# Front of a two-layer recurrent kernel: layernorm tiles and MLP steps issued in written order, decays one turn later, one more MLP step in each pass over the chunks' products

## The chip, the cores and the metric

The kernel runs on one core of a Trainium2 chip. Its engines are TensorE (PE in the profile, with PEld for its weight loads), VectorE (DVE), ScalarE (ACT), GpSimd (POOL) and SyncE (SP), which here only issues transfers. The metric is the time of one execution on the device in microseconds (us), taken as the median of several runs; less is better.

## The reference, cut to what matters

Two layers run on an input x of 2 x 1024 tokens with 512 features, in float32. Only the first layer is touched:

```python
xn = _layernorm(x)
# attention: 16 heads of 128, q, k, v through a causal convolution of 4 taps and silu
q, k, v = (silu(conv(xn @ W)) for W in (Wq, Wk, Wv))
alpha, beta = sigmoid(xn @ Wa + ba), sigmoid(xn @ Wb + bb)
S = alpha * S - beta * ((S k - v) k^T);  o = S q      # step by step over the tokens
s = (layernorm(o) * ln_w + ln_b) * sigmoid(xn @ Wg) @ Wo
# MLP: 512 -> 1408 -> 512
g = silu((silu(xn @ gate_w.T * gate_s) * (xn @ up_w.T * up_s)) @ down_w.T * down_s)
x = x + s * g
```

The second layer (another recurrence and a larger MLP) starts from this x.

## The kernel before, in words

The tokens are 16 tiles of 128 rows (`NTT`). The first layer has three parts, which follow each other in the code of `first_layer`.

**Layernorm (from L368).** Each tile of x is loaded by SP, `layernorm` (L74) puts statistics, mean and variance (`st`, `mv`, `ve`) on DVE, the power -1/2 (`rs`) on POOL, and the normalised tile `xn` on DVE again. `transposed` (L105) turns it on PE with the identity in `cst` and copies it by ACT into `xnT`, which holds all tokens with the features on the partitions. Between the tiles, `mlp_weights` (L351) loads the MLP's weights `gwT`, `uwT`, `dwT` from POOL's queue in four parts, kept in order there: chunk 0 ahead of the tiles, 1 and 2 after tile 3, 3 to 6 after tile 5, 7 to 10 after tile 7.

**The front (to L940).** Two things run beside each other.
- `mlp` (L399) is a generator. For each of four blocks of 512 tokens it splits `xnT` into a high and a low part (`xh` by ACT, `xl` by DVE) and then takes 11 chunks of 128 hidden features: 8 matmuls into `pg`, 8 into `pu`, `sg` (silu, ACT), `hd` (DVE), `hh` (ACT), `hl` (DVE), and 8 matmuls of the chunk before into the four banks `po`. A twelfth call of a block holds the last `po` alone; the next call starts with the block's result `g` and its store in `gd`. `some(n)` takes n calls; there are 48.
- The heads of the first three groups of two heads (`hg`) are prepared. `z` and `softplus` (L482 to L507) give the decays' logarithms, which are stored as rows in `gr` and `egr`. Then, for each `hg` and each of four windows `p` of 256 tokens of both sequences: `ahead_k` projects the keys with `wk` and convolves them (`pwk`, `ka`); `ahead_e` loads two chunks' rows of `gr` into the tile `e`, adds the mask (DVE) and takes eight exponentials (ACT), then stores `e`; `ell` calls `ahead_l` for the two chunks of the window before, four products of keys each (`pkk`), times `e` (`lt`, DVE), stored in `dl`; 14 steps of `invert` (DVE) of the group before.

**The heads' loop (from L985).** 64 units of two heads' chunks; what comes ahead of it are the loads of `wq`, `wv` and `wg` for two groups (`load_weights`, on SP), the first projections, and `within`, which loads `kb`, `ground`, `eb`, `eg`. From `order["loop"] = True` on, everything is issued in written order, with `later(n, ...)` to delay a step by n slots.

What sets the order: outside that loop, a planner in the compiler lays out each engine's queue ahead of the run. At each point of its own estimate of time it takes, of what it holds to be ready, what was written first. An engine then works its queue strictly in that order, and waits where an input is late. `keep_in_program_order` pins an instruction behind the one written before it for its engine, and the class `Ordered` does so with all calls on an engine while a condition holds. `issue_after` queues what a block writes for one engine behind a given instruction. Rooms of tiles (`tile_pool`) are used again once their last reader is done; those of the front, closed by `front.close()`, become those of the loop: `ground`, then the working tiles, then the weights.

In the code before, the order around the change is: 16 layernorm tiles; small loads; 11 MLP steps by `some(IC)`; `z` and decays; 12 turns with two MLP steps each; the rest of the MLP:

```python
        for p in range(NP):
            some(1)
            done(ahead_k(hg, p, wk["wk"], stores[hg]))
            ahead_e(hg, p, stores[hg])
            some(1)
            ell()
            for _ in zip(range(0 if hg and not p else 14), steps):
                pass
            ls.append((hg, p))
    ell()
    some(NTT * IC)
    front.close()
```

Of the kernel before, what the change touches and what calls it, by code (L numbers as in the profile page):

```python
# [22 lines left out]
P = 128  # L23
# [4 lines left out]
H = 16  # L28
# [44 lines left out]

def layernorm(nc, pool, out, in_, minus_half, eps=EPS):  # L74

    st = pool.tile([P, 6], F32, tag="ln_st", name="ln_st")
    nc.vector.bn_stats(st, in_)
    mv = pool.tile([P, 2], F32, tag="ln_mv", name="ln_mv")
    nc.vector.bn_aggr(mv, st)
    ve = pool.tile([P, 1], F32, tag="ln_ve", name="ln_ve")  # L80
    nc.vector.tensor_scalar(ve, mv[:, 1:2], eps, None, ALU.add)
    rs = pool.tile([P, 1], F32, tag="ln_rs", name="ln_rs")
    nc.gpsimd.tensor_tensor(rs, ve, minus_half[:, 0:1], ALU.pow)
    nc.vector.tensor_scalar(out, in_, mv[:, 0:1], rs, ALU.subtract, ALU.mult)

# [206 lines left out]
def first_layer(ctx, tc, a, cst, minus_half, keep, xnT, od, gd, pd, then):  # L292
# [74 lines left out]

    mlp_weights(0, 1)  # L368
    with tc.tile_pool(name="ln0", bufs=3) as lp:
        for ti in range(NTT):  # L370
            xt = lp.tile([P, D], F32, tag="xt", name=f"x_{ti}", bufs=7)
            nc.sync.dma_start(xt, a["x"][ti * P : (ti + 1) * P, :])
            xn = lp.tile([P, D], F32, tag="xn", name=f"xn_{ti}")
            layernorm(nc, lp, xn, xt, minus_half)
            b, t0 = ti // NC, (ti % NC) * P
            transposed(nc, pools["a"], ("pa", "pi")[ti % 2], xnT[:, :, b, t0 : t0 + P], xn, ident, "scalar")
            if ti in (3, 5, 7):
                mlp_weights(*{3: (1, 3), 5: (3, 7), 7: (7, IC)}[ti])

    gus = fx.tile([P, 2, IC], F32, name="gus")  # L380
    nc.sync.dma_start(gus, a["gus"])
    dsc = fx.tile([P, D], F32, name="dsc")
    nc.sync.dma_start(dsc, a["dsc0"].unsqueeze(0).to_broadcast([P, D]))
    cw = cp.tile([P, 3, H, 4], F32, name="cw")
    nc.sync.dma_start(cw, a["cw"])
    cb = cp.tile([P, 3, H], F32, name="cb")
    nc.sync.dma_start(cb, a["cb"])
    lnwb = cp.tile([P, 2], F32, name="lnwb")
    nc.sync.dma_start(lnwb, a["lnwb"])

    nc.vector.tensor_scalar(lnwb, lnwb, 0.5, None, ALU.mult)

    pl = early.enter_context(tc.tile_pool(name="at_l", bufs=1, reuse_waits="tile"))
    wab = pl.tile([P, KC, 2 * H], F32, name="wab")
    nc.sync.dma_start(wab, a["wab"].rearrange("(kc p) n -> p kc n", p=P))
    bab = pl.tile([2 * H, 1], F32, name="bab")
    nc.sync.dma_start(bab, a["bab"].unsqueeze(1))

    def mlp():  # L399

        for tt in range(NT // TB):
            b, t0 = tt // 2, (tt % 2) * TB
            xs = []
            for kc in range(KC):
                src = xnT[:, kc, b, t0 : t0 + TB]
                xh = fx.tile([P, TB], F32R, tag=f"xh{kc}", name=f"xh_{tt}_{kc}")
                nc.scalar.copy(xh, src)
                xl = fx.tile([P, TB], F32R, tag=f"xl{kc}", name=f"xl_{tt}_{kc}")
                nc.vector.tensor_tensor(xl, src, xh.bitcast(F32), ALU.subtract)
                xs.append((xh, xl))  # L410
# [4 lines left out]
            for ic in range(IC + 1):  # L415
                was = hs
                if ic < IC:
                    pgu = []
                    for n, wt in (("g", "gwT"), ("u", "uwT")):
                        pp = ps_h.tile([P, TB], F32, tag=f"p{n}", name=f"p{n}_{tt}_{ic}")  # L420
                        for kc in range(KC):
                            for i, part in enumerate(xs[kc]):
                                nc.tensor.matmul(  # L423
                                    pp,
                                    lhsT=mw[wt, ic][:, kc, :],
                                    rhs=part,
                                    start=(kc == 0 and i == 0),
                                    stop=(kc == KC - 1 and i == 1),
                                )
                        pgu.append(pp)  # L430
                    sg = ft.tile([P, TB], F32, tag="sg", name=f"sg_{tt}_{ic}")
                    nc.scalar.activation(sg, pgu[0], AF.Silu, scale=gus[:, 0, ic : ic + 1])
                    hd = ft.tile([P, TB], F32, tag="hd", name=f"hd_{tt}_{ic}")
                    nc.vector.scalar_tensor_tensor(
                        hd, in0=pgu[1], scalar=gus[:, 1, ic : ic + 1], in1=sg,
                        op0=ALU.mult, op1=ALU.mult,
                    )
                    hh = ft.tile([P, TB], F32R, tag="hh", name=f"hh_{tt}_{ic}")
                    nc.scalar.copy(hh, hd)
                    hl = ft.tile([P, TB], F32R, tag="hl", name=f"hl_{tt}_{ic}")  # L440
                    nc.vector.tensor_tensor(hl, hd, hh.bitcast(F32), ALU.subtract)
                    hs = (hh, hl)
                if was is not None:
                    for tl in range(TB // P):
                        for i, part in enumerate(was):
                            nc.tensor.matmul(  # L446
                                po[tl],
                                lhsT=part[:, tl * P : (tl + 1) * P],
                                rhs=mw["dwT", ic - 1],
                                start=(ic == 1 and i == 0),  # L450
                                stop=(ic == IC and i == 1),
                            )
                yield
            for tl in range(TB // P):
                ti = tt * (TB // P) + tl
                g = ft.tile([P, D], F32, tag="g", name=f"g_{ti}", bufs=4)
                nc.vector.tensor_tensor(g, po[tl], dsc, ALU.mult)
                last["act"] = nc.scalar.activation(g, g, AF.Silu)
                nc.scalar.dma_start(gd[ti * P : (ti + 1) * P, :], g)
# [7 lines left out]

    def load_weights(hg, names):
        w = {}
        for n in names:  # L470
            pool = pools["w"] if n != "wk" else kp if "b" in pools or not hg else fz
            w[n] = pool.tile([P, KC, 2 * P], F32, tag=n, name=f"{n}_{hg}")
            nc.sync.dma_start(
                w[n], a[n][:, hg * 256 : (hg + 1) * 256].rearrange("(kc p) n -> p kc n", p=P)
            )
        return w
# [3 lines left out]
    NCOL = NC * H * B  # L480
    some(IC)
    z = fz.tile([P, 2, NC, H, B], F32, name="z")  # L482
# [162 lines left out]
    def ahead_e(hg, p, store):  # L645
# [13 lines left out]

        def exps(i, streams):  # L660
            e, c = es[i], 2 * p + i
            col = c * H * B + hg * NS
            for s in streams:
                ACT.activation(
                    e[:, s, 1 : P + 1], e[:, s, 1 : P + 1], AF.Exp, bias=bcol[:, col + s : col + s + 1]
                )
            if s == NS - 1:
                nc.sync.dma_start(store["e"][c], e[:, :, 1 : P + 1])

        later(0, lambda: load(2 * p), lambda: load(2 * p + 1))  # L670
        later(5, lambda: masked(0), lambda: masked(1))
        later(8, *(functools.partial(exps, i, (s,)) for i in range(2) for s in range(NS)))

# [245 lines left out]
    def ell():  # L919
        if ls:  # L920
            hg, p = ls.pop(0)
            for c in (2 * p, 2 * p + 1):
                done(ahead_l(hg, c, stores[hg]))

    for hg in range(3):
        stores[hg] = new_store(hg)
        wk = load_weights(hg, ("wk",))
        steps = invert(hg - 1, stores[hg - 1]) if hg else iter(())
        for p in range(NP):
            some(1)  # L930
            done(ahead_k(hg, p, wk["wk"], stores[hg]))
            ahead_e(hg, p, stores[hg])
            some(1)
            ell()
            for _ in zip(range(0 if hg and not p else 14), steps):
                pass
            ls.append((hg, p))
    ell()
    some(NTT * IC)
    front.close()  # L940
    last_w = ctx.enter_context(ExitStack())
# [43 lines left out]
    with tc.issue_after(last["act"].ins):  # L985
        for hg in range(2):
            weights[hg] = load_weights(hg, ("wq", "wv", "wg"))
        done(made(0, 0, "q"))
# [49 lines left out]
        def joined():  # L1038
# [3 lines left out]
            later(1, *joining.rest())  # L1042

        before, joining, late, ls, steps = none, None, none, [], none
        order["loop"] = True
        for u in range(len(units) + 1):
# [40 lines left out]
            if turn4 in (0, 2) and ls:  # L1087
                hg, i_ = ls[turn4 // 2]
                later(7 if turn4 == 0 else 2, functools.partial(ahead_e, hg, i_, stores[hg]))
            if turn4 == 0:  # L1090
# [495 lines left out]
def body(ctx, tc, a, out):  # L1586
    nc = tc.nc
    keep = ctx.enter_context(tc.tile_pool(name="keep", bufs=1))
    cst = keep.tile([P, 3, P], F32, name="cst")
    nc.sync.dma_start(cst, a["consts"])  # L1590
    minus_half = keep.tile([P, NS], F32, name="minus_half")
# [94 lines left out]
```

## Time and profile before

| | |
|---|---|
| median of 3 runs | 3205.46 us (3205.04 to 3208.45) |
| the profiled execution, its own time | 3207.82 us |
| its span, first to last instruction | 3206.0 us |
| PE busy | 3154.4 us (98%) |
| DVE, ACT, POOL busy | 2145.9, 1249.3, 829.2 us |
| first transpose on PE | 12.73 us |
| first matmul of the MLP | 17.79 us |
| first matmul of `z` (in the chain) | 88.72 us |
| first projection of the loop (`pwq`) | 412.04 us |
| x loads, median from issue to landing | 5.8 us |
| `e<-gr`, median from issue to landing, whole run | 4.1 us |
| mean granted PE clock | 0.995 |

The profile is one execution; its instructions carry the line of the kernel or of a helper (L131 is the call inside `Ordered`, so there the names of tiles tell more than the line). An entry reads: start, duration, engine, line, operation, out<-in, shape, and in brackets how long the engine stood idle ahead of it and who released it. PEclk is the clock that PE was granted, as a share of full speed. The times of matmuls overlap, since they are pipelined and their ends are modelled; what counts is the distance from one group to the next.

### The profile page before, as it was taken

To read this page: it belongs to the slowest core of one execution; us is meant where nothing else is said; L and a number is where in the kernel's file an instruction comes from. 1 tells how busy PE (TensorE), PEld (TensorE's weight loads), DVE (VectorE), ACT (ScalarE), POOL (GpSimd) and SP (SyncE) were. 2 spreads that over 40 slices of the span, in tenths; PEclk is the share of its full clock that TensorE was granted. 3 is DMA by queue.
4 is the path that set the end of the run, shared out by engine and by line. 5 is a ranking of instruction groups with operands and counts; after the bars stand their busy time and mean duration, and the time that the engine had idled before them with its cause. 6 is when DMAs were issued, how large, how long until landed. Compare 5 with 4: busy or idle time off the path is not lost.

```text
span 3206.0 us, 38256 instructions
## 1 busy us (share of the span) xinstructions
PE 3154.4 (98%) x12454; PEld 1953.3 (61%) x12454; DVE 2145.9 (67%) x4294; ACT 1249.3 (39%) x2267; POOL 829.2 (26%) x1204
## 2 busy tenths in 40 slices
PE   7999999999999999999999999999999999999998
PEld 6566756666666666666666644555555555555554
DVE  4566568787777868675554454676777666776677
ACT  3475445555555555434333300322222222322223
POOL 2000022222222222222222210333233333333222
PEclk9999999999999999999999999999999999999999
DMA  6244333444444543444334365110001100110014
GB/s 182 63 138 113 98 103 96 117 133 127 124 113 121 147 120 98 117 126 104 96 90 135 108 191 163 35 38 27 27 27 33 33 27 27 33 33 27 27 36 131
DMA packets 501798, 287.40 MB, mean 90 GB/s; under 512 B 207328, under 2 KB 443616, under 8 KB 501600
## 3 DMA queue, kind: packets, MB, share of 16 engines
q1 hardware_dynamic: 493600, 272.12, 30.2%
q0 software_dynamic: 5696, 8.65, 0.9%
q10 hardware_dynamic: 2304, 4.20, 0.4%
q8 instruction: 99, 1.62, 0.2%
q14 instruction: 99, 0.81, 0.1%
HBM read 183.90 MB, written 88.34 MB: 85 GB/s over the span
## 4 chain that ended last, share of the span: by engine, by line
PE 87%; DVE 5%; DMA 3%; ACT 2%; issue 2%; SPq 1%; POOL 0%; DVEq 0%; ACTq 0%; POOLq 0%
PE po L131 15%; PE pua L131 7%; PE pga L131 7%; PE pgate L131 6%; PE pwk L131 6%; PE pwq L131 5%; PE pwv L131 5%; PE zw L131 4%; PE pgc L131 3%; PE puc L131 3%; PE jpo L210 3%; PE pg L423 2%; PE pu L423 2%; PE po L446 2%; PE pub L131 2%
## 5 line engine op out<-in xcount | busy, mean ns | idle before, releaser
L131 DVE TENSOR_TENSOR acc<-acc,po 128x512 f32<-128x512 f32 x408 | 278.3, 682 | 208.3 <-PE po L131 207.6
L131 PEld LDWEIGHTS po<-w_d,i 128*128 128x128 f32 x1024 | 194.5, 190 | 142.6 <-issue 111.2
L131 PE MATMUL po<-w_d,i 128*128 128x256 f32 (+1 forms) x1024 | 275.3, 392 | 0.0
L131 PE MATMUL pgate<-xnT,wg 128*128 128x512 f32 x512 | 245.7, 593 | 0.0
L131 PE MATMUL pwq<-xnT,wq 128*128 128x512 f32 x512 | 245.1, 593 | 0.0
L131 PE MATMUL pwv<-xnT,wv 128*128 128x512 f32 x512 | 243.0, 593 | 1.8 <-ACT gate L131 1.8
L131 PE MATMUL pua<-xq,w_u 128*128 128x512 f32 x512 | 240.6, 592 | 0.0
L131 PE MATMUL pga<-xq,w_g 128*128 128x512 f32 x512 | 240.6, 592 | 0.0
L131 PE MATMUL pwk<-xnT,wk 128*128 128x512 f32 x512 | 238.0, 595 | 1.7 <-ACT ka L131 1.7
L131 ACT COPY g<-pga 128x512 f32<-128x512 f32 x96 | 56.2, 585 | 447.3 <-PE pga L131 447.3
L131 DVE SCALAR_TENSOR_TENSOR v<-prewv,cw,v 128x512 f32<-128x512 f32 x192 | 169.0, 881 | 63.2 <-ACT v L131 53.8
L131 PEld LDWEIGHTS po<-w_d,s 128*128 128x128 f32 x720 | 136.8, 190 | 95.4 <-issue 77.2
L131 ACT COPY w<-zw 128x128 f32<-128x128 f32 x192 | 50.6, 264 | 359.5 <-PE zw L131 359.5
L131 DVE TENSOR_TENSOR rr<-rr,zw 128x128 f32<-128x128 f32 x192 | 54.8, 285 | 198.1 <-PE zw L131 196.6
L131 PE MATMUL po<-w_d,s 128*128 128x256 f32 x720 | 184.8, 379 | 0.0
L131 POOL TENSOR_TENSOR ot<-ot,gate 128x512 f32<-128x512 f32 x64 | 86.6, 1354 | 344.3 <-ACT ot L131 314.9
L131 POOL TENSOR_TENSOR rs<-rs,minus_half 128x4 f32<-128x4 f32 x64 | 64.4, 1007 | 428.9 <-DVE rs L131 389.9
L131 DVE SCALAR_TENSOR_TENSOR ka<-prewk,cw,ka 128x512 f32<-128x512 f32 x192 | 147.9, 772 | 36.7 <-ACT ka L131 25.7
L131 PEld LDWEIGHTS zw<-rr,ground 128*128 128x128 f32 x512 | 96.8, 191 | 123.8 <-issue 101.6
L131 DVE SCALAR_TENSOR_TENSOR q<-prewq,cw,q 128x512 f32<-128x512 f32 x192 | 159.1, 829 | 13.8 <-ACT q L131 7.3
L131 ACT ACT_TABLE_LOAD x115 | 147.5, 1283 | 14.5 <-PE pr L131 11.3
L131 PEld LDWEIGHTS zw<-w,ground 128*128 128x128 f32 x768 | 111.3, 192 | 65.7 <-issue 54.4
(249 smaller groups left out, 6686.3 us busy)
## 6 DMA issues: line engine op xcount, KB each, us to landing
e<-gr SPq DMA_DIRECT2D x64, 256.0 KB, 4.1
de<-e SPq DMA_DIRECT2D x64, 256.0 KB, 2.7
dk<-ka SPq DMA_DIRECT2D x32, 512.0 KB, 2.8
kb<-dk SPq DMA_DIRECT2D x64, 256.0 KB, 3.4
eb<-de SPq DMA_DIRECT2D x64, 256.0 KB, 3.0
eg<-egr SPq DMA_DIRECT2D x64, 256.0 KB, 3.8
od<-ot SPq DMA_DIRECT2D x64, 256.0 KB, 2.1
wt<-w SPq DMA_DIRECT2D x768, 16.0 KB, 1.9
```

The costliest lines, as they stand in the source:

```text
L131: i = getattr(self.engine, name)(*args, **kw)
L210: matmul(po, lhsT=ot[:, h, :], rhs=self.wo[h], start=(h == h0), stop=(h == H - 1))
L423: nc.tensor.matmul(pp, lhsT=mw[wt, ic][:, kc, :], rhs=part, start=(kc == 0 and i == 0), stop=(kc == KC - 1 and i == 1),)
L446: nc.tensor.matmul(po[tl], lhsT=part[:, tl * P : (tl + 1) * P], rhs=mw["dwT", ic - 1], start=(ic == 1 and i == 0), stop=(ic == IC and i == 1),
```

## The change

Five things are done in `first_layer`; `body` only gives up its load of `cst`.

1. The layernorm's tiles and the first 11 MLP steps go through `Ordered`, so on PE, DVE, ACT and POOL they are issued as written. `layernorm` now returns its last operation (`xn`) for the caller to place: for tiles 0 to 3 it comes after the statistics of the next tile, for the others at once. From tile 4 on, each tile but the last is followed by one MLP step (`some(1)`) and then by its transposes. x is loaded two tiles ahead in the text; `cst` comes after the first two tiles, `gus` and `dsc` after the fourth; the other small loads stay behind the tiles.
2. `ahead_e` returns its loads, masks and exponentials as lists. In the front the loads are done in their turn, the masks and exponentials at the start of the next turn. In the loop `decays` places them as before.
3. `ell` takes one MLP step between the two halves, and one more comes after the last turn.
4. The first six weight loads of the loop (`wq`, `wv`, `wg` of two groups) are issued from POOL instead of SP.
5. The halving of `lnwb` is pinned behind the front on DVE.

```diff
-def layernorm(nc, pool, out, in_, minus_half, eps=EPS):
+def layernorm(vector, gpsimd, pool, out, in_, minus_half, eps=EPS):
...
-    nc.vector.tensor_scalar(out, in_, mv[:, 0:1], rs, ALU.subtract, ALU.mult)
+    return lambda: vector.tensor_scalar(out, in_, mv[:, 0:1], rs, ALU.subtract, ALU.mult)
...
+    first = {"on": True}
+    ordered = {
+        n: Ordered(tc, getattr(nc, n), lambda: first["on"])
+        for n in ("tensor", "vector", "scalar", "gpsimd")
+    }
...
-                nc.scalar.copy(xh, src)
+                ordered["scalar"].copy(xh, src)
...
+        xts = [load_x(ti) for ti in range(2)]
+        nc.sync.dma_start(cst, a["consts"])
+        mlp_weights(0, 1)
+
+        late = None
+        for ti in range(NTT):
+            if ti + 2 < NTT:
+                xts.append(load_x(ti + 2))
+            xn, end = normed(ti, xts[ti])
+            if ti < 4:
+                if late:
+                    turned(*late)
+                late = ti, xn, end
+                if ti == 3:
+                    turned(*late)
+                    gus = fx.tile([P, 2, IC], F32, name="gus")
+                    nc.sync.dma_start(gus, a["gus"])
+                    dsc = fx.tile([P, D], F32, name="dsc")
+                    nc.sync.dma_start(dsc, a["dsc0"].unsqueeze(0).to_broadcast([P, D]))
+            else:
+                end()
+                if ti < NTT - 1:
+                    some(1)
+                turned(ti, xn, lambda: None)
+            if ti in (3, 5, 7):
+                mlp_weights(*{3: (1, 3), 5: (3, 7), 7: (7, IC)}[ti])
...
-    some(IC)
+    first["on"] = False
...
-        later(0, lambda: load(2 * p), lambda: load(2 * p + 1))
-        later(5, lambda: masked(0), lambda: masked(1))
-        later(8, *(functools.partial(exps, i, (s,)) for i in range(2) for s in range(NS)))
+        return (
+            [lambda: load(2 * p), lambda: load(2 * p + 1)],
+            [lambda: masked(0), lambda: masked(1)],
+            [functools.partial(exps, i, s) for i in range(2) for s in range(NS)],
+        )
...
                 done(ahead_l(hg, c, stores[hg]))
-
+                if c == 2 * p:
+                    some(1)
+
+    of_e = ()
...
         for p in range(NP):
+            for step in of_e:
+                step()
             some(1)
             done(ahead_k(hg, p, wk["wk"], stores[hg]))
-            ahead_e(hg, p, stores[hg])
+            loads, *of_e = ahead_e(hg, p, stores[hg])
+            of_e = itertools.chain(*of_e)
+            for step in loads:
+                step()
             some(1)
             ell()
...
+    for step in of_e:
+        step()
+    some(1)
     ell()
     some(NTT * IC)
+
+    tc.keep_in_program_order(nc.vector.tensor_scalar(lnwb, lnwb, 0.5, None, ALU.mult))
     front.close()
...
-            weights[hg] = load_weights(hg, ("wq", "wv", "wg"))
+            weights[hg] = load_weights(hg, ("wq", "wv", "wg"), nc.gpsimd)
...
+        def decays(hg, p):
+            for n, some_steps in zip((0, 5, 8), ahead_e(hg, p, stores[hg])):
+                later(n, *some_steps)
```

More of the change, by code (lines that the diff above doesn't have):

```diff
@@ L71, in rep @@
     return ap.unsqueeze(1).to_broadcast([ap.shape[0], n, ap.shape[1]])
-def layernorm(nc, pool, out, in_, minus_half, eps=EPS):
+def layernorm(vector, gpsimd, pool, out, in_, minus_half, eps=EPS):
     st = pool.tile([P, 6], F32, tag="ln_st", name="ln_st")
-    nc.vector.bn_stats(st, in_)
+    vector.bn_stats(st, in_)
     mv = pool.tile([P, 2], F32, tag="ln_mv", name="ln_mv")
-    nc.vector.bn_aggr(mv, st)
+    vector.bn_aggr(mv, st)
     ve = pool.tile([P, 1], F32, tag="ln_ve", name="ln_ve")
-    nc.vector.tensor_scalar(ve, mv[:, 1:2], eps, None, ALU.add)
+    vector.tensor_scalar(ve, mv[:, 1:2], eps, None, ALU.add)
     rs = pool.tile([P, 1], F32, tag="ln_rs", name="ln_rs")
-    nc.gpsimd.tensor_tensor(rs, ve, minus_half[:, 0:1], ALU.pow)
-    nc.vector.tensor_scalar(out, in_, mv[:, 0:1], rs, ALU.subtract, ALU.mult)
+    gpsimd.tensor_tensor(rs, ve, minus_half[:, 0:1], ALU.pow)
+    return lambda: vector.tensor_scalar(out, in_, mv[:, 0:1], rs, ALU.subtract, ALU.mult)
 def softplus(nc, pool, out, x, sign, tags):
@@ L366, in mlp_weights @@
             mw["dwT", ic] = w[:, ic - c0, :]
[L368 to L397, printed above, removed]
+    first = {"on": True}
[3 more added lines that the diff above has]
+    }
     def mlp():
@@ L406, in mlp @@
                 xh = fx.tile([P, TB], F32R, tag=f"xh{kc}", name=f"xh_{tt}_{kc}")
-                nc.scalar.copy(xh, src)
+                ordered["scalar"].copy(xh, src)
                 xl = fx.tile([P, TB], F32R, tag=f"xl{kc}", name=f"xl_{tt}_{kc}")
-                nc.vector.tensor_tensor(xl, src, xh.bitcast(F32), ALU.subtract)
+                ordered["vector"].tensor_tensor(xl, src, xh.bitcast(F32), ALU.subtract)
                 xs.append((xh, xl))
@@ L422, in mlp @@
                             for i, part in enumerate(xs[kc]):
-                                nc.tensor.matmul(
+                                ordered["tensor"].matmul(
                                     pp,
@@ L431, in mlp @@
                     sg = ft.tile([P, TB], F32, tag="sg", name=f"sg_{tt}_{ic}")
-                    nc.scalar.activation(sg, pgu[0], AF.Silu, scale=gus[:, 0, ic : ic + 1])
+                    ordered["scalar"].activation(sg, pgu[0], AF.Silu, scale=gus[:, 0, ic : ic + 1])
                     hd = ft.tile([P, TB], F32, tag="hd", name=f"hd_{tt}_{ic}")
-                    nc.vector.scalar_tensor_tensor(
+                    ordered["vector"].scalar_tensor_tensor(
                         hd, in0=pgu[1], scalar=gus[:, 1, ic : ic + 1], in1=sg,
@@ L438, in mlp @@
                     hh = ft.tile([P, TB], F32R, tag="hh", name=f"hh_{tt}_{ic}")
-                    nc.scalar.copy(hh, hd)
+                    ordered["scalar"].copy(hh, hd)
                     hl = ft.tile([P, TB], F32R, tag="hl", name=f"hl_{tt}_{ic}")
-                    nc.vector.tensor_tensor(hl, hd, hh.bitcast(F32), ALU.subtract)
+                    ordered["vector"].tensor_tensor(hl, hd, hh.bitcast(F32), ALU.subtract)
                     hs = (hh, hl)
@@ L445, in mlp @@
                         for i, part in enumerate(was):
-                            nc.tensor.matmul(
+                            ordered["tensor"].matmul(
                                 po[tl],
@@ L456, in mlp @@
                 g = ft.tile([P, D], F32, tag="g", name=f"g_{ti}", bufs=4)
-                nc.vector.tensor_tensor(g, po[tl], dsc, ALU.mult)
-                last["act"] = nc.scalar.activation(g, g, AF.Silu)
+                ordered["vector"].tensor_tensor(g, po[tl], dsc, ALU.mult)
+                last["act"] = ordered["scalar"].activation(g, g, AF.Silu)
                 nc.scalar.dma_start(gd[ti * P : (ti + 1) * P, :], g)
@@ L466, in some, with load_x, normed, turned @@
             pass
-    def load_weights(hg, names):
+    with tc.tile_pool(name="ln0", bufs=3) as lp:
+        def load_x(ti):
+            xt = lp.tile([P, D], F32, tag="xt", name=f"x_{ti}", bufs=7)
+            nc.sync.dma_start(xt, a["x"][ti * P : (ti + 1) * P, :])
+            return xt
+        def normed(ti, xt):
+            xn = lp.tile([P, D], F32, tag="xn", name=f"xn_{ti}")
+            return xn, layernorm(ordered["vector"], ordered["gpsimd"], lp, xn, xt, minus_half)
+        def turned(ti, xn, last):
+            last()
+            b, t0 = ti // NC, (ti % NC) * P
+            transposed(types.SimpleNamespace(**ordered), pools["a"], ("pa", "pi")[ti % 2], xnT[:, :, b, t0 : t0 + P], xn, ident, "scalar")
+        xts = [load_x(ti) for ti in range(2)]
[23 more added lines that the diff above has]
+                mlp_weights(*{3: (1, 3), 5: (3, 7), 7: (7, IC)}[ti])
+    cw = cp.tile([P, 3, H, 4], F32, name="cw")
+    nc.sync.dma_start(cw, a["cw"])
+    cb = cp.tile([P, 3, H], F32, name="cb")
+    nc.sync.dma_start(cb, a["cb"])
+    lnwb = cp.tile([P, 2], F32, name="lnwb")
+    nc.sync.dma_start(lnwb, a["lnwb"])
+    pl = early.enter_context(tc.tile_pool(name="at_l", bufs=1, reuse_waits="tile"))
+    wab = pl.tile([P, KC, 2 * H], F32, name="wab")
+    nc.sync.dma_start(wab, a["wab"].rearrange("(kc p) n -> p kc n", p=P))
+    bab = pl.tile([2 * H, 1], F32, name="bab")
+    nc.sync.dma_start(bab, a["bab"].unsqueeze(1))
+    def load_weights(hg, names, queue=nc.sync):
         w = {}
@@ L472, in load_weights @@
             w[n] = pool.tile([P, KC, 2 * P], F32, tag=n, name=f"{n}_{hg}")
-            nc.sync.dma_start(
+            queue.dma_start(
                 w[n], a[n][:, hg * 256 : (hg + 1) * 256].rearrange("(kc p) n -> p kc n", p=P)
@@ L658, in masked, with exps @@
             DVE.tensor_tensor(e[:, :, 1 : P + 1], e[:, :, 1 : P + 1], rep(mask, NS), ALU.add)
-        def exps(i, streams):
+        def exps(i, s):
             e, c = es[i], 2 * p + i
             col = c * H * B + hg * NS
[L663 to L666, printed above, removed]
+            ACT.activation(
+                e[:, s, 1 : P + 1], e[:, s, 1 : P + 1], AF.Exp, bias=bcol[:, col + s : col + s + 1]
+            )
             if s == NS - 1:
                 nc.sync.dma_start(store["e"][c], e[:, :, 1 : P + 1])
-        later(0, lambda: load(2 * p), lambda: load(2 * p + 1))
-        later(5, lambda: masked(0), lambda: masked(1))
-        later(8, *(functools.partial(exps, i, (s,)) for i in range(2) for s in range(NS)))
+        return (
+            [lambda: load(2 * p), lambda: load(2 * p + 1)],
+            [lambda: masked(0), lambda: masked(1)],
+            [functools.partial(exps, i, s) for i in range(2) for s in range(NS)],
+        )
     def ahead_l(hg, c, store):
@@ L1088, in first_layer @@
                 hg, i_ = ls[turn4 // 2]
-                later(7 if turn4 == 0 else 2, functools.partial(ahead_e, hg, i_, stores[hg]))
+                later(7 if turn4 == 0 else 2, functools.partial(decays, hg, i_))
             if turn4 == 0:
@@ L1589, in body @@
     cst = keep.tile([P, 3, P], F32, name="cst")
-    nc.sync.dma_start(cst, a["consts"])
     minus_half = keep.tile([P, NS], F32, name="minus_half")
```

## Prediction, made before the change was run

> **What bounds the kernel now.** The page has TensorE (PE) busy for 98% of the span, so a gain can come only from stretches in which PE stands still or runs slow. All of the change lies ahead of the heads' loop, and that begins at 412.04 us, with the first projection by `wq`. So I asked first for the busy time of the engines in the stretches up to 412, cut where the chain shows a new kind of work:
>
> ```profile
> core 0: us, PE busy (x) PEld busy (x) DVE busy (x) ACT busy (x) POOL busy (x), PEclk, DMA share, GB/s
> 0.00:88.70 88.70, 71.82 (x321) 56.92 (x322) 40.89 (x93) 29.89 (x48) 20.28 (x41) 0.98 0.56 165
> 88.70:320.00 231.30, 229.56 (x894) 149.94 (x894) 141.60 (x243) 142.63 (x234) 13.11 (x62) 1.00 0.40 109
> 320.00:356.00 36.00, 29.46 (x107) 20.74 (x106) 29.44 (x68) 21.77 (x40) 0.00 (x0) 0.81 0.36 108
> 356.00:412.00 56.00, 56.00 (x241) 44.87 (x240) 21.62 (x45) 14.61 (x23) 3.45 (x5) 1.00 0.29 71
> ```
>
> The first and the third stretch have idle PE, and the third has a granted clock of 0.81. The ends of matmuls are modelled, so I count work instead of trusting busy time. The chain of work gives the pace of each kind where nothing waits (start, us, what):
>
> ```profile
> 55.18 1.86 PE pg L423 x8
> 57.04 1.87 PE pu L423 x8
> 58.91 1.85 PE po L446 x8
> ...
> 93.76 3.55 PE pz L488 x8
> ...
> 166.60 6.87 PE pwk L131 x16
> ...
> 219.01 0.89 PE pkk L131 x8
> ```
>
> So an MLP step is 1.86 + 1.87 + 1.85 = 5.58, one `ahead_k` 6.87, one `pkk` tile 0.89, all `pz` 4 x 3.55 = 14.2; the timeline has the transposes of two tiles in 1.03, so 0.52 a tile. Work by stretch, from the matmuls that each holds (tile queries for pg, pu, po, pwk, pkk, 8 or 16 to a group as in the chain):
> - to 88.7: 11 pg/pu pairs (41.0), 10 po (18.5), 16 tiles (8.2) = 67.7. Lost: 21.0, of which 12.7 ahead of the first transpose.
> - to 320: 21 steps (117.2), pz and what hangs on it (17), 11 `ahead_k` (75.6), 20 pkk (18) = 228. Lost: 3.5.
> - to 356: 24 + 17 + 18 matmuls of the MLP (13.7), 1 `ahead_k` (6.9), 4 pkk (3.6) = 24.2. Lost: 11.8.
> - to 412: ten steps of pure MLP, 56.0. Lost: nothing.
>
> Together 36 us. The waits of the first 130 us, then of 130 to 412 (total, times, longest), say on whom:
>
> ```profile
> DVE ln_st L77 <- DMA x<-in_x: 16.5, 8, 4.4
> PE ptr L114 <- DVE xn L84: 13.6, 2, 12.7
> ```
> ```profile
> PE po L446 <- DVE hl L441: 2.8, 1, 2.8
> ```
>
> VectorE's (DVE's) own timeline shows why the first transpose is at 12.7:
>
> ```profile
> 5.09 0.18 DVE L79 BATCH_NORM_AGGREGATE ln_mv<-ln_st 128x2 f32<-128x6 f32 x1
> 7.30 0.69 DVE L77 BATCH_NORM_STATS2 ln_st<-x 128x6 f32<-128x512 f32 x1 [2.03 <-DMA x<-in_x]
> 7.92 0.14 DVE L81 TENSOR_SCALAR ln_ve<-ln_mv 128x1 f32<-128x1 f32 x1
> ...
> 12.14 1.44 DVE L84 TENSOR_SCALAR xn<-x,ln_mv,ln_rs 128x512 f32<-128x512 f32 x3
> ```
>
> Tile 0 has its mean and variance at 5.3, but the planner put the next tiles' statistics ahead of its `ve` and `xn`: the queue stands behind transfers that landed later than planned.
>
> **Part 1, layernorm and the first 11 steps in written order.** Queue of DVE, with the durations above (stats 0.69, aggregate 0.18, `ve` 0.14, `xn` 0.54, POOL's power 0.55): stats 0 at 4.3, `ve` 0 by 5.4, stats 1 at 6.9 (x_1 is now issued ahead of `cst`; it landed at 7.3), `xn` 0 done by 8.5, then 1.56 a tile: `xn` 3 done at 12.3. POOL then issues three weight loads (2.4 us in this trace, at 14.50 to 16.88) ahead of the power of tile 4, so `xn` 4 ends at 15.4; it stands ahead of `xl` on DVE. `xl` 0 ends at 16.1 and the MLP starts there, against 17.79 now. Its first pg and pu are 3.7 us of work. Here a rule matters. The clock: rows of this trace grant 0.50 at 20 to 22 us and 0.72 at 22 to 24, though PE had worked since 12.7. The Trainium skill, "TensorE: Matmul & The Clock Gate", Part 1, says that the array starts at half rate and is freed after about 3.4 us of sustained work. By the rule, PE is freed before 20 and pg/pu end at 22.4; by the row (five slow microseconds after the MLP starts) they end nearer 23.5. I take 22.4, and 23.5 for the range. From there ten turns of 5.58 + 0.52, and two more tiles: 84.5. A turn's other engines fit: DVE 0.75 + 0.69 + 1.55 = 3.0 us of 6.1; ScalarE (ACT) 0.69 + 0.62 + 0.58 = 1.9. `xn` of the next tile is ready 4.6 us after pu, its transposes come 8.5 after. The weights for steps 3 to 6 are issued after the power of tile 5, at about 24, and needed at 33 (gate) and 35 (up): at 390 GB/s (the rate at 26 to 42 us now) 1 MB takes 2.7 us, so they land at about 29.5 and 32; the 13.8 and 16.4 us to landing of now are with both big sets and x under way at once. **Gain: 88.7 - 84.5 = 4.2**, between 1 and 7.
>
> **Part 2, MLP steps spread, and decays a turn later.** Before, 11 steps, then two in each of 12 turns, then the other 13 calls (the generator has 48, four of them only a po) in one block. After, `ell` takes one between its two halves, and nothing is left for the block. No work is added. What moves: the 11.8 us of 320 to 356, where the last `ahead_k`, the second inversion, the last masks and exponentials and the block change of the MLP (new `xh`, `xl`, four `g`) fell together with DVE 82% busy and PE out of order only by plan. After, the last block change comes in the first turn of the third group of heads, which has no inversion steps; and behind the last `ahead_k` stand three steps, 16.8 us, where the chain from it to `pkk` is 5 us (0.6 + 0.8 copies, 3 x 0.75 taps, 1.06 silu). A turn is 6.87 + 3 x 5.58 + 1.78 = 25.4 us of PE, against about 21 of DVE. The masks (24 x 0.69), exponentials (96 x 0.39) and table loads (1.28) are the same in number; their place a turn later keeps DVE from standing behind `e<-gr` (6.6 us of waits in 130 to 412), but the 3.5 us lost from 88.7 to 320 bound what that brings, and I count nothing. The last turn's masks now come after the loop, and the end has only one step and a po as cover, so I leave 4 us lost there (1 to 12). **Gain: 11.8 - 4 = 8.** With it goes the clock: 0.50 was granted from 338 to 350 after PE waited.
>
> **Part 3, the six weight loads of the loop go from SP's queue to POOL's.** SP now:
>
> ```profile
> 375.63 0.76 SPq L473 DMA_DIRECT2D wq<-in_wq  x1
> ...
> 414.79 0.37 SPq L473 DMA_DIRECT2D wg<-in_wg  x1
> ```
>
> Five of six are issued by 381, 31 us ahead of use, so their room is free long before the last step; the sixth waits 33.6 us for the last stores of `g` and holds up SP, with `kb` and `ground` behind it. On POOL it holds up the memsets of `pre` and `eg` and the halo copies, which the loop's first taps need 5 us later than PE's first 6.87 us: covered. The Trainium skill, "DMA: Bandwidth & Descriptors", section "SWDGE vs HWDGE vs iDMA", speaks against it: plain copies belong on SP or ACT, whose setup is faster. The rows agree on the sign (512 KB: 5.5 us to landing from SP, 7.1 and more from POOL; issue 0.37 and 0.86). With cover the rule costs nothing; without, 2 us. SP freed early brings at most the 1.3 us that PE idles from 430 to 500. **Together: 0.5 lost** (-1 to +3). The moved `lnwb` (0.36 us of DVE), `cst`, `gus`, `dsc` and small loads lie under the same cover: 0.
>
> **Sum.** 4.2 + 8 - 0.5 = 11.7. The profiled execution took 3207.8 (span 3206.0); 3207.8 - 11.7 = 3196.1, and the median of the runs is 2.4 lower: **3193.8**. From 412 on the order is the same and only shifts. About 0.2% (6.4 us) can be told from no change, so "same" is 3199 to 3212.
>
> **Rivals.**
> - *The first stage gains nothing* (12%): x arrivals rule it, for which the 16.5 us of waits speak; against it, most fall after 25 us, when the planner had run ahead of the transfers. 3193.8 + 4.2 = 3198.
> - *The end keeps its stall* (16%): the planner still lays out masks and `pkk` by its own landing times; it pulls MLP steps forward while the decays are not ready, and the end is bare. For it: DVE waits on `e<-gr` in every turn now. 3193.8 + 8 = 3202, no change.
> - *Slower* (12%): at the switch to the loop, the weight loads stand on POOL behind `ground`'s memset (3.31 us, released at 408.31 by the last pu) and behind the last stores of `g`, which the sixth load waited for (414.79). Then `wq` lands at 414.8 + 1.0 + 7 to 9.6 = 423 to 425: 11 to 13 us of idle PE and, by the 12 us at 0.50 above, 6 more. 3193.8 + 19 = 3213. It breaks even at 11.7, and is slower beyond 18. Against it: five loads didn't wait so.
> - *Likeliest* (60%): 3187 to 3199.
>
> Range 3185 (startup 7, end 1, loop's start 1.3) to 3207 (over the stall's case, part of the loads'). Faster 0.72, same 0.16, slower 0.12.
>
> **What would show it.** First transpose near 9 and `pz` from 82 to 87; no stretch of over 3 us with PE idle between there and the end of the front; last po near 400; `wq` landed before that. Wrong if PE waits for gwT or uwT in turns 2 to 4, if DVE's `e` masks stand between hd and hl while PE waits, or if the first pwq comes later than 2 us after the last MLP matmul.

## The result, and the profile after

The changed kernel takes 3190.24 us (median of 6 runs, 3187.01 to 3192.71), the kernel before 3206.86 us in the same comparison (6 runs, 3205.04 to 3210.47): a ratio of 0.9949, with a 95% interval of 0.9939 to 0.9959. That is 16.6 us faster, where the forecast was 11.7. The profiled execution took 3191.48 us, with a span of 3188.9. The loop starts at 392.9 us instead of 412.0, so 19.1 us had been won there; 17.1 are left in the span. The first 120 us of the loop hold about as much idle PE as before (2.1 us against 2.0), and the last 2 us are no more than two profiles of one kernel differ by (3188.9 and 3186.3 for the changed kernel).

The same view as before, busy time in stretches, cut at the first `pz` (88.4) and at the first `pwq` (392.9):

```profile
core 0: us, PE busy (x) PEld busy (x) DVE busy (x) ACT busy (x) POOL busy (x), PEclk, DMA share, GB/s
0.00:88.40 88.40, 77.56 (x344) 61.42 (x344) 47.02 (x98) 32.72 (x53) 20.66 (x41) 1.00 0.58 172
88.40:320.00 231.60, 230.10 (x896) 153.18 (x896) 140.20 (x238) 140.62 (x235) 11.51 (x52) 1.00 0.36 99
320.00:356.00 36.00, 36.00 (x156) 27.00 (x155) 29.86 (x68) 19.30 (x32) 1.74 (x9) 1.00 0.28 87
356.00:392.90 36.90, 36.90 (x167) 28.13 (x166) 21.70 (x43) 18.70 (x30) 6.88 (x7) 1.00 0.43 110
```

The third stretch had 29.46 us of busy PE at a clock of 0.81; it now has 36.00 at 1.00, and nothing is left idle from there to the loop. Counted as work with the durations of the forecast: up to `pz` there are 12 pg/pu pairs (44.8), 11 po (20.4) and 16 tiles (8.2), so 15.1 us are lost of 88.4 (before 21.0). `pz` itself starts no earlier than before, because one more pair and po stand ahead of it. From `pz` to the loop there are 32 pairs (119.4), 33 po (61.1), `pz` and what hangs on it (17), 12 `ahead_k` (82.4) and 24 `pkk` (21.4), 301.3 together, so 3.2 us are lost of 304.5 (before 3.5 + 11.8). The two parts have won 5.9 and 12.1; the 1.1 us to 19.1 are within the rounding of these durations.

The start on DVE and PE (timelines of each):

```profile
3.40 0.69 DVE L132 BATCH_NORM_STATS2 ln_st<-x 128x6 f32<-128x512 f32 x1 [3.40 <-DMA x<-in_x]
...
4.42 0.68 DVE L132 BATCH_NORM_STATS2 ln_st<-x 128x6 f32<-128x512 f32 x1
...
5.42 0.54 DVE L132 TENSOR_SCALAR xn<-x,ln_mv,ln_rs 128x512 f32<-128x512 f32 x1
7.89 0.69 DVE L132 BATCH_NORM_STATS2 ln_st<-x 128x6 f32<-128x512 f32 x1 [1.93 <-DMA x<-in_x]
```
```profile
6.56 1.09 PE L132 MATMUL ptr<-cst,xn 128*128 128x128 f32 x4 [6.56 <-DMA cst<-in_consts]
...
14.45 0.80 PE L132 MATMUL pg<-xh,gwT 128*128 128x512 f32 x1 [1.32 <-ACT xh L132]
15.46 0.79 PE L132 MATMUL pg<-xl,gwT 128*128 128x512 f32 x1 [0.22 <-DVE xl L132]
...
19.04 0.58 PE L132 MATMUL pu<-xl,uwT 128*128 128x512 f32 x1
19.46 0.40 PE L132 MATMUL pu<-xh,uwT 128*128 128x512 f32 x1
...
20.87 0.60 PE L132 MATMUL ptr<-cst,xn 128*128 128x128 f32 x4
```

The first transpose now waits for the identity, not for statistics; it comes at 6.56 instead of 12.73, the MLP at 14.45 instead of 17.79, and the first step ends at 20.87. From there a turn takes 6.0 us, up to the last at 81.10. Of the 15.1 us still lost, 12.4 lie ahead of the MLP's first matmul (14.45 less four tiles of 0.52) and 2.7 in the first step (6.42 against 3.73 of work).

The switch to the loop, on POOL and on SP:

```profile
375.34 0.80 POOL L505 DMA_DIRECT2D wq<-in_wq  x1 [15.97 <-ACT sg L132]
376.13 0.77 POOL L505 DMA_DIRECT2D wv<-in_wv  x1
387.69 3.30 POOL L995 MEMSET ground<- 128x3840 f32 x1 [10.79 <-PE pu L132]
390.94 0.75 POOL L505 DMA_DIRECT2D wg<-in_wg  x1
```
```profile
384.63 14.13 SPq L720 DMA_DIRECT2D dl<-lt  x12
402.21 0.59 SPq L732 DMA_DIRECT2D ll<-dl  x1
```

`wq` and `wv` are out 17 us ahead of use. The other four loads do stand behind the memset of `ground`, as the slower rival had it, but the loop needs them last. SP meanwhile issues stores of `lt` from 384.6 to 398.8. This line turned out to be the one that matters.

### The profile page after: what moved, and what is told of

The parts are those of the page before. It is cut to its first block, busy times and chain, and to the rows that moved or that the text cites. A ratio compares the mean times of both kernels' runs of the same rounds, so it can differ in the third digit from the quotient of the medians.

```text
span 3188.9 us, 38235 instructions
## 1 busy us (share of the span) xinstructions
PE 3148.8 (99%) x12454; PEld 1950.8 (61%) x12454; DVE 2147.2 (67%) x4294; ACT 1251.4 (39%) x2269; POOL 832.4 (26%) x1210
## 4 chain that ended last, share of the span: by engine, by line
PE 76%; DVE 5%; issue 2%; ACT 1%; DMA 1%; SPq 1%; POOL 0%; DVEq 0%; ACTq 0%; POOLq 0%
PE po L132 15%; PE pua L132 7%; PE pga L132 7%; PE pgate L132 6%; PE pwq L132 5%; PE pwv L132 5%; PE pwk L132 4%; PE zw L132 4%; PE pgc L132 3%; PE puc L132 3%; PE jpo L211 3%; PE pub L132 2%; PE pgb L132 2%; PE pr L132 2%; PE pks L132 1%
```

## The experiments

The theory (A): the start and the stall are separate gains that add; the decays' place and the queue of the six loads are worth about nothing. Rivals: the stall is an accident of the plan, which any change ahead of it dissolves (C), or the decays' later place, not the spread steps, takes the stall away (B). Each run is set beside runs of the kernel before that were taken with it.

### The start alone

Before, with `layernorm`, x loads, transposes and 11 steps as in item 1 of the change (and item 5), nothing else:

```diff
+    first = {"on": True}
+    ordered = {n: Ordered(tc, getattr(nc, n), lambda: first["on"]) ...}
...
-    some(IC)
+    first["on"] = False
```

> The kernel before with the layernorm and the first 11 MLP steps in written order, nothing else of the change but the place of the lnwb halving. Theory A (two separate gains: the start of PE, and the MLP steps spread so that no stretch is left without cover): only the start is gained. Time lost by PE up to the first pz falls from 21.0 to about 15 us, the stall between 320 and 356 stays: 6 us faster than before, 3201. Rival C (the stall of 320 to 356 was an accident of the plan, which any change ahead of it dissolves): 18 us faster, 3189.

Measured: 3199.69 us against 3206.34, 0.9977 (0.9968 to 0.9987): 6.6 us faster. The stall stays, in the stretches of 20 us:

```profile
320.00:340.00 20.00, 14.34 (x62) 10.66 (x60) 15.75 (x35) 16.88 (x33) 0.00 (x0) 0.91 0.52 129
340.00:360.00 20.00, 18.20 (x69) 14.66 (x70) 16.31 (x40) 5.89 (x10) 0.00 (x0) 0.83 0.29 78
```

C falls: the start is a gain of its own, of the size that the trace of the whole change shows (5.9).

### The MLP steps spread, alone

The kernel before with item 3 of the change only (`spread_only`):

```diff
                 done(ahead_l(hg, c, stores[hg]))
+                if c == 2 * p:
+                    some(1)
...
+    some(1)
     ell()
```

> The kernel before with one MLP step more in each ell and one behind the last turn, nothing else. Theory A: the start stays (first transpose at 12.7, 21 us lost to the first pz), the front's stall goes: 12 us faster than before, 3195. Rival B (the gain of the second half comes from the masks and exponentials a turn later, which keep DVE from standing behind their loads): no change, 3207. Rival C gives 12 here too.

Measured: 3203.38 us, 0.9991 (0.9984 to 0.9997): 3.0 us, a quarter of what was expected. Yet the stall is gone: PE is busy for 20.00 us in both stretches from 320 to 360. The time is lost again at the loop's start, on PE and on SP:

```profile
397.14 1.05 PE L131 MATMUL pkk<-ka 128*128 128x128 f32 x8
406.15 9.15 PE L131 MATMUL pwq<-xnT,wq 128*128 128x512 f32 x16 [7.96 <-DMA wq<-in_wq]
```
```profile
396.26 6.27 SPq L687 DMA_DIRECT2D dl<-lt  x8
402.64 0.39 SPq L473 DMA_DIRECT2D wq<-in_wq  x1
```

PE's last work of the front begins at 397.1, and `wq`, issued by SP only after the stores of `lt`, lands at 406.2. The projection then takes 9.15 us instead of 7.03 (its time in the changed kernel), at a granted clock of 0.50:

```profile
404.00:408.00 4.00, 1.85 (x2) 0.84 (x3) 0.00 (x0) 0.00 (x0) 0.00 (x0) 0.50 1.02 330
```

7.96 + 2.1 = 10.1 us go there. A's last clause falls. In its place (A2): the spread steps and POOL's queue belong together.

### POOL's queue alone, and both together

```diff
-            weights[hg] = load_weights(hg, ("wq", "wv", "wg"))
+            weights[hg] = load_weights(hg, ("wq", "wv", "wg"), nc.gpsimd)
```

> The kernel before with only the six weight loads moved to POOL. By theory A2 the queue matters only where the MLP steps are spread, since in the kernel before five of six were issued 31 us ahead of use: no change, 3206 to 3208, the stall of 320 to 356 in place. The prediction's sum gave 0.5 us more. If POOL's queue is worth something by itself (SP no longer held 33.6 us by the sixth load): up to 1.3 us less.

> The kernel before with one MLP step more in each ell and one behind the last turn, and the six weight loads on POOL; layernorm and decays as before. Theory A2: the stall of the front is gone and wq is there in time: 3206.3 - 12 = 3194. Rival (the decays a turn later are needed too): wq in time but a stall of 5 us or more in the last turns: 3199 or more. If only the queue was wrong in spread_only, PE's wait of 8.0 us for wq must be gone.

POOL alone: 3209.7 us, 1.0009 (1.0001 to 1.0017), 3.3 us slower; its first `pwq` is at 411.9, as before, so nothing is late there. Its profile has the span of the kernel before, 3206.0; where the 3 us go stays open. Both: 3192.97 us against 3207.59, 0.9958 (0.9946 to 0.9971), 14.6 faster. `pwq` starts at 398.75 and PE's only wait from 130 to 420 is 1.4 us for `ka`. So the two changes gain -3.3 and +3.0 us alone and +14.6 together: A2 holds.

### The whole change with the loads back on SP

```diff
-            weights[hg] = load_weights(hg, ("wq", "wv", "wg"), nc.gpsimd)
+            weights[hg] = load_weights(hg, ("wq", "wv", "wg"))
```

> The changed kernel with the six weight loads of the loop back on SP's queue. Theory A2 (formed after spread_only: the MLP steps and the POOL queue belong together, since with the steps spread the stores of lt fill SP's queue to the end of the front and wq is issued behind them): wq lands some 8 us after the last matmul of the front, PE waits and comes back at half clock: 3190 + 11 = 3201. Theory of the prediction (the queue is worth 0.5 us either way, its room being free early): 3190.

Measured: 3193.96 us, 0.996 (0.9946 to 0.9974), 3.7 and 5.9 us above the changed kernel's two medians (3190.24, 3188.09), and 7.4 above `warm` (3186.58, below), which was measured together with it and has the loads on POOL; not 11. PE waits 4.24 us for `wq`, which SP gets to issue between two groups of stores:

```profile
384.86 8.30 SPq L720 DMA_DIRECT2D dl<-lt  x8
393.26 0.39 SPq L505 DMA_DIRECT2D wq<-in_wq  x1
394.40 3.16 SPq L720 DMA_DIRECT2D dl<-lt  x4
```
```profile
397.58 8.83 PE L132 MATMUL pwq<-xnT,wq 128*128 128x512 f32 x16 [4.24 <-DMA wq<-in_wq]
```

The mechanism is the one of A2, with a smaller price: `wq` was issued one group of stores earlier, so the wait is about half as long. The clock fell here too, only for less time: 0.50 is granted from 399 to 401, and the projection takes 8.83 us instead of 7.03. 4.24 + 1.8 = 6.0 us go there.

### The whole change without the spread steps

```diff
-                if c == 2 * p:
-                    some(1)
...
-    some(1)
```

> The changed kernel without the MLP step in ell and without the one behind the last turn; the start in written order, the decays a turn later and the weight loads on POOL stay. Theory A: a stall comes back in the front's last turns, and a block of pure MLP follows it: 10 to 12 us slower than the changed kernel, 3201. Rival B: no change against the changed kernel, 3190. Rival C: no change either.

Measured: 3205.18 us, 0.9993 (0.9984 to 1.0001), 15 to 17 us above the changed kernel. The stall is back (14.84 and 18.28 us busy from 320 to 360, clock 0.89 and 0.77), and now it is `lt` that PE waits for:

```profile
PE pkk L132 <- DVE lt L132: 6.0, 3, 3.5
```

This kernel is also 5.5 us slower than the start alone, though it only adds the decays' later place and POOL's queue. Alone these cost 2.3 and 3.3. Over all runs the stall follows the spread steps: the eight profiles with them have PE busy for all 40 us from 320 to 360, the five without them for 32 to 33.5.

### The decays a turn later, alone, and back in their turn

Before with item 2 of the change only (`decays_only`):

> The kernel before with only the masks and exponentials a turn later. Theory A: nothing gained, since the stall stays where the MLP steps give no cover, 3205 to 3209. Rival B: the stall goes, 12 us faster, 3195, with the waits of DVE on e<-gr (8 us in the front) near zero. Rival C: the plan changes here too, so about 12 faster.

Measured: 3208.61 us, 1.0005 (0.9997 to 1.0014). The stall is only moved, from a wait for `hl` to one for `lt`, which reads exponentials that now come later (waits of 130 to 420, then the stretches):

```profile
PE pkk L131 <- DVE lt L131: 6.3, 3, 3.6
```
```profile
320.00:340.00 20.00, 17.60 (x71) 11.79 (x70) 19.36 (x44) 15.01 (x25) 0.00 (x0) 1.00 0.32 89
340.00:360.00 20.00, 14.51 (x57) 10.78 (x56) 14.90 (x38) 10.86 (x21) 0.00 (x0) 0.83 0.53 140
```

B falls. The other way round, the whole change with masks and exponentials in their own turn:

```diff
-            loads, *of_e = ahead_e(hg, p, stores[hg])
-            of_e = itertools.chain(*of_e)
-            for step in loads:
+            for step in itertools.chain(*ahead_e(hg, p, stores[hg])):
                 step()
```

> The changed kernel with each turn's masks and exponentials in its own turn. Theory A2: their place is worth nothing or costs, as decays_only said (3208.6 against 3206.3): 3188 to 3191, PE losing at most 4 us between the first pz and the first pwq. Rival B: 5 us or more of PE waits come back in the front, 3195 or more.

Measured: 3187.04 us, 0.9938 (0.9925 to 0.995). That is no slower than the changed kernel (0.9949 and, run again, 0.9939); PE is busy throughout from 320 to the loop, and DVE only 9.79 us of the 20 from 320 on. The later place brings nothing. Against the changed kernel's medians it seems to cost 1 to 3 us; against `warm` (below), measured together with this run and with the later place, it costs nothing (3186.58). These runs can't tell.

### A warm PE at the start

The changed kernel with a few matmuls of ones (dummies), which nobody reads, in PE's gaps of the first 13 us (`warm`). The expectation's "page" is the one on the clock that the prediction cites.

```diff
+        wz = ft.tile([P, TB], F32, tag="sg", name="wz")
+        ordered["vector"].memset(wz, 1.0)
+        wp = ps_h.tile([P, TB], F32, tag="pg", name="wp")
...
+                ordered["tensor"].matmul(wp, lhsT=wz[:, :P], rhs=wz, start=True, stop=True)
```

> The changed kernel with six matmuls of ones more on PE, three ahead of the first transpose, two behind the second tile's and one behind the fourth's, whose result nobody reads. The first MLP step took 6.4 us (14.45 to 20.87) in the changed kernel, ten of its matmuls at 0.43 us. By the page's rule of a clock freed after some 3.4 us of sustained work, they run at 0.23 us now and the step ends by 19.7: 1.2 us less in the profile, too little for the medians (3189 to 3190). By the rival (the clock is not what holds the step, its inputs xh and xl are): it ends at 20.9 as before.

Measured: 3186.58 us, 0.9939 (0.9927 to 0.9951). The first step ended at 20.09, 0.8 earlier than in the changed kernel and 0.4 later than expected, and by the interval no gain is shown. The matmuls of the MLP start at full pace, 0.26 to 0.34 us apart, and fall to 0.43 at 15.87; the stretches show the clock:

```profile
12.00:14.00 2.00, 1.23 (x3) 0.19 (x1) 0.64 (x3) 1.97 (x4) 1.43 (x3) 1.00 1.07 340
14.00:16.00 2.00, 1.33 (x5) 0.73 (x6) 2.00 (x5) 1.98 (x3) 0.00 (x0) 0.99 1.18 323
16.00:18.00 2.00, 2.00 (x5) 1.58 (x6) 0.42 (x1) 0.52 (x2) 0.00 (x0) 0.50 1.24 345
```

From 12.7 to 14.7, between its last dummy and the first `xl`, PE did a single matmul (0.49 us); the clock was lowered about a microsecond after that gap, when PE had full work again. The last kernel puts dummies into that gap too, and has the decays in their turn:

> The changed kernel with each turn's masks and exponentials in its own turn and with eight matmuls of ones between the first transposes (three ahead of them, two after the first tile's, one after the second's, two after the fourth's). In warm the clock fell back to 0.50 at 16 us, after PE had idled at 12.7 to 14.7; with the denser row it should stay at 1.00 and the first MLP step end near 18.8 (20.9 in the changed kernel, 20.1 in warm). Sum: decays in turn 3 us, clock 2 us: 5 us under the changed kernel, 3185. If the masks' place was noise: 3188.

> The changed kernel once more, on the same chip as the next two, as their measure: 3190, as before (3187 to 3193).

Measured together: 3186.33 us, 0.9933 (0.9921 to 0.9946), and the changed kernel 3188.09 us, 0.9939 (0.9925 to 0.9952). Here the pace stays full (timeline of PE):

```profile
14.57 0.47 PE L132 MATMUL pg<-xh,gwT 128*128 128x512 f32 x1
15.55 0.50 PE L132 MATMUL pg<-xl,gwT 128*128 128x512 f32 x1 [0.51 <-DVE xl L132]
...
19.33 0.40 PE L132 MATMUL pu<-xl,uwT 128*128 128x512 f32 x1
19.56 0.60 PE L132 MATMUL ptr<-cst,xn 128*128 128x128 f32 x4
20.70 0.47 PE L132 MATMUL pg<-xh,gwT 128*128 128x512 f32 x1 [0.54 <-DMA gwT<-in_gwT]
```

The step ends at 19.56, 1.3 us earlier, not at 18.8 as expected, because `xl` comes as late as before. So the cold clock costs 1.3 us of the first step, but this kernel doesn't keep them. The second step waits for its weights, 0.54 us for `gwT` and 1.26 for `uwT`, and ends at 27.87, where the changed kernel's ends at 26.88; `pz` starts at 89.4 instead of 88.4. From the second step on, the transfers hold the start back in this profile, not the clock. 1.8 us less than the changed kernel is the lowest median of the study, but the intervals overlap, and the first steps don't explain it.

## Why the prediction held, and where it failed

**Part 1 (4.2 expected; 5.9 by the trace, 6.6 alone).** The mechanism was right: DVE's queue no longer stands behind late statistics. Three terms were mis-sized.

- The arrival of x. x_1 was counted to land at 6.9; issued ahead of `cst` it landed with x_0 (statistics at 3.40 and 4.42). But x_2 came only at 7.89, so `xn` 4 keeps 0.6 us of that lead (14.81, counted 15.4). The MLP starts at 14.45, not 16.1, mostly because its first matmul needs `xh` alone; the first with `xl` is at 15.46.
- The clock. The forecast read five slow microseconds after the MLP's start out of the rows of before. That was a misreading: there the MLP's first matmuls go at full pace (0.23 to 0.34 us apart from 18.71 to 19.78, granted 1.00 up to 19), and the slow stretch comes later, from 19.7 to 23.1, after PE had stood still from 16.5 to 17.8. In the changed kernel the matmuls do run at half pace from the first one on, for 5.0 us, 4.0 of them after the last gap (15.46 to 19.46), against the 3.4 that the Trainium skill, "TensorE: Matmul & The Clock Gate", Part 1, gives for sustained work. The step took 6.4 us, counted 6.3 by the rule and 7.4 by the row; its end at 20.87 instead of 22.4 is owed to the earlier start.
- The weights for steps 3 to 6. Counted to land at 29.5 and 32, they landed at 31.7 (`gwT`) and 34.7 (`uwT`). That was no wait, but only by half a microsecond: `uwT` is first used at 35.22.

The turns of 6.1 held (6.0). `pz` was expected from 82 to 87 and came at 88.4, since the forecast left out the pair and the `po` that now stand ahead of it (3.73 + 1.85); that moves work and loses none.

**Part 2 (8 expected; 12.1 by the trace).** The 11.8 us of the stall went, and of the 4 us left for a bare end nothing came; the other 3.5 became 3.2. Taking the stall for a matter of cover (too few MLP steps beside the chain through DVE) fits the runs: the whole change without the spread steps brings it back, the spread alone removes it. The decays, "I count nothing", brought nothing; alone they made `pkk` wait for `lt`, so that the place needs the spread steps as cover.

**Part 3 (0.5 lost expected; by the traces it is worth 6 in the whole change and 10 beside the spread alone).** This is the step that failed: "Five of six are issued by 381, 31 us ahead of use, so their room is free long before the last step." This is true of the order before only. There a block of pure MLP, 56 us with few stores, ended the front, and SP reached the loads early. With the steps spread, `ell` works up to the end, SP issues stores of `lt` until PE has done its last step, and a load written behind them comes 8 us (spread alone) or 4 us (whole change) too late; the lower clock after the wait costs 2 us more. The second part created the need for the third, and by costing them one by one on the queue of before I missed it. That the sum still came out is luck: the change contains both, so the missing term never showed. The rule that the prediction set against the move (plain copies belong on SP or ACT) speaks of setup; POOL alone, 3.3 us slower, agrees with it in sign, though where these 3 us go is open. In the whole change it pointed the wrong way: the place in the queue, 4 to 8 us of PE's wait, weighed more than the 0.4 us of issue and the few us of landing.

**The sum.** The start alone 6.6, spread with POOL 14.6, decays -2.3 (not clear of noise): 18.9 if they add; measured 16.6 and, the second time, 18.3. It fits within the few us by which these medians vary.

**The rivals.** The start that gains nothing and the end that keeps its stall didn't come. The slower one had the place right (four loads behind `ground`'s memset) and the consequence wrong: `wq` and `wv` were taken early, and the last four are needed only behind 7 us each of projections.

## What to carry to other kernels

Before a move of work is costed, lay out anew each queue that the moved steps write to: a load that was early behind a quiet stretch is late when the stretch fills with stores, and the engine with the slower issue but an empty queue can then be the better one. Here a stall of the critical engine beside a long chain on another was cured by spreading independent work over the turns, not by a later place for part of the chain. Test such parts alone and in pairs: -3.3 and +3.0 alone were +14.6 together.

## What was not expected of the hardware

The granted clock in the profile seems to miss the cold start. In the changed kernel its stretches from 14 to 20 us say 1.00 while the MLP's matmuls start 0.43 us apart; after 19.46 the same matmuls are 0.23 apart. In the run with dummies the same pace of 0.43 stands beside a granted 0.50. In the kernel before, 16 transposes at 12.73 take 3.73 us under a granted 1.00, as slow as eight at 20.21 under 0.50 (1.91 us). At the start of a kernel the distance between matmuls is the surer reading.

A gap also takes the clock away late: in the run with dummies, after some 2 us of mostly idle PE (12.7 to 14.7), the pace halved at about 15.9, in the middle of dense work, and was full again at about 19.4. The same lag stands in the kernel before (gap from 16.5 to 17.8, low from 19.7) and with the loads back on SP (gap from 393.3 to 397.6, low from 398.3). Worked out from rows of one microsecond (with the loads back on SP 0.65, 0.50, 0.50 and 0.64 from 398 to 402, so low from 398.3 to 401.7), the low stretch lasts 3.4 us in each of these three, 6.8 after the wait for `wq` with the spread alone (403.4 to 410.2), and 13.6 in the stall of before (337.2 to 350.8): one, two and four times 3.4. So a wait of PE can cost more than its own length; the two waits for `wq` cost about 2 us more.
